# Runs of indirect scatters with a wait on GpSimd after every fourth

## The chip, the cores and the metric

The kernel runs on one core of a Trainium2 chip. A core has TensorE (matmul, PE in the profile, its weight loads PEld), VectorE (DVE), ScalarE (ACT), GpSimd (POOL) and SyncE (SP), which issues plain DMAs; all DMAs share 16 engines. The metric is the time of one execution on the device, in microseconds. Before the change it is 320.58 us, the median of three runs (319.81 to 322.14).

## The reference

A layer norm of `x` (16 rows of 512 tokens, 128 features each) feeds two branches, and both are added to `x`: a linear attention with a decay, and a mixture of four different experts of which each token uses two. Cut to what matters:

```python
xn = layernorm(x)
# attention
q, k, v = xn @ q_w, xn @ k_w, xn @ v_w              # 32 features each
scores = (q @ k.T) * decay ** max(diff - 1, 0) * (diff > 0)
attn = (scores @ v) @ o_w.T * out_scale
# experts
logits = xn @ router_w + router_b + load_balancer
rw, sel = top_k(logits, 2);  rw = softmax(rw)
e0 = silu(xn @ w1) * (xn @ w3) @ w2
e1 = gelu(((xn @ eq) @ wv @ wo) @ c1w) @ c2w         # with biases
e2 = two layer norms around a relu network, then gen_w
e3 = gelu(xn @ ml_w1) @ ml_w2
out = x + attn + sum(rw * chosen two experts)
```

All in float32.

## The kernel before

**Staging.** In the first stage the 16 rows of x are taken in six groups of 1, 1, 2, 4, 4 and 4 rows (`GROUPS`). For each row VectorE takes the moments, GpSimd makes the inverse standard deviation (`inverse`, L465, a `pow`), VectorE an offset (L470), ScalarE normalizes each 128-token chunk into a buffer `pay` (L475), TensorE transposes (L482), and so on through the projections and the attention. The sum of x and attention is stored to the output straight away by SyncE (`store`, L584).

**Lists.** Each token picks a pair of experts, and there are six pairs. A token's normalized row with its two weights and its own number (131 floats) is sent to the list of its pair in device memory, a table called `lists`. That is done by `Group.send`: an indirect DMA of GpSimd for each chunk of 128 tokens, 64 in all, each with 128 row numbers from a column of `idx`.

**Tiles.** In the second stage 21 tiles of at most 512 tokens of one pair (`LISTS`, `TURN`) are loaded from the lists (`load`, SyncE, L857, which waits for the last scatter of its group), transposed, passed through the two experts on TensorE with ScalarE and VectorE behind it, and summed into a buffer `o` (four of them; first written by `biases`, L885 and L887, and added to by `joined`, L939). Then `Tile.send` scatters each chunk of `o` with accumulation to the rows of the output whose numbers are in the tile's `to` (L871): 66 more indirect DMAs of GpSimd. Expert 2 has two layer norms, whose `pow` is on GpSimd too (`rstd_u`, `rstd_v`).

Both kinds of scatter go through one helper, `scatter`, and so appear on one line of the profile, L487. The kernel declares that two scatters into the same table do not depend on each other, so a scatter does not wait for the one before it.

**Order.** Every step is entered with `add(name, engine, us, fn, after, takes, rank)`: an assumed duration, what it must follow, which buffers it takes. `emit` then runs a small plan: it keeps for each engine the time from which it is free, picks the step that can start first (among those that start within 0.25 us of it on the same engine, the one of lowest rank), and issues its instructions. This fixes the order on TensorE, VectorE, ScalarE and SyncE; GpSimd's instructions follow the same plan through the helper `queued`. The plan chooses the PSUM banks and the buffers too. Names of steps that begin with `s` on GpSimd are the list scatters (`send0.0` and so on, 1.28 us by the plan), those with `X` the output scatters (1.87 us). A buffer that a scatter reads is free for others `LATE` us after the scatter's planned end.

At the end a count is taken that decides whether a slow path for overfull lists is run; with these inputs it is not.

Of the kernel before, what the change touches and what calls it, by code (L numbers as in the profile page):

```python
# [83 lines left out]
def decay_attention__plus__routed_experts(  # L84
# [10 lines left out]
    nc = tc.nc  # L95
# [17 lines left out]
        "h2T": 1, "z2T": 1, "o": 4,  # L113
    }

    LATE = {"x": 3.0, "o": 3.2, "pay1": 2.6, "pay2": 2.6}


# [25 lines left out]
    def queued(i, key=None):  # L144

        if queue["on"]:
            others = [q for q, k in queue["moving"] if k != key or key is None]
            for q in others or [queue["fixed"]]:
                if q is not None:
                    tc.add_manual_dep(i.ins, q, behind, reason="the order of the plan")  # L150
            if key:
                queue["moving"].append((i.ins.name, key))
            else:
                queue.update(fixed=i.ins.name, moving=[])
        return i
# [7 lines left out]
    PE, V, A, G, S = "PVAGS"  # L163
# [7 lines left out]
    def emit():  # L171
        free = dict.fromkeys("PVAGS", 0.0)
        slots = {kind: [()] * n for kind, n in ROOM.items()}
        slots["x"] = [(f"store{b}",) for b in range(ROOM["x"])]
        done, left = {}, {n: len(p[3]) for n, p in plan.items()}
        followers = {}
        for n, p in plan.items():
            for q, _ in p[3]:
                followers.setdefault(q, []).append(n)
        ready = [n for n in plan if not left[n]]  # L180
        while ready:
            starts = {}
            for n in ready:
                eng, us, fn, after, takes, rank, at = plan[n]
                t = max(at, free[eng])
                for q, lat in after:
                    if lat is None:
                        lat = 0.05 if plan[q][0] == eng else 0.2
                    t = max(t, done[q] + lat)
                for kind in {k for k, _ in takes}:  # L190
                    ends = sorted(
                        max((done[q] for q in s), default=-1.0) + LATE.get(kind, 0.2)
                        for s in slots[kind] if all(q in done for q in s)
                    )
                    count = sum(k == kind for k, _ in takes)
                    t = max(t, ends[count - 1]) if len(ends) >= count else None
                    if t is None:
                        break
                if t is not None:
                    starts[n] = t  # L200
            assert starts, f"no step can go on: {ready}"
            first = min(starts, key=starts.get)
            eng, soon = plan[first][0], starts[first] + 0.25
            n = min(
                (m for m in starts if plan[m][0] == eng and starts[m] <= soon),
                key=lambda m: (plan[m][5], starts[m]),
            )
            eng, us, fn, after, takes, rank, at = plan[n]
            for kind, users in takes:
                i = min(  # L210
                    (i for i, s in enumerate(slots[kind]) if all(q in done for q in s)),
                    key=lambda i: max((done[q] for q in slots[kind][i]), default=-1.0),
                )
                slots[kind][i] = (n, *users)
                given.setdefault((kind, n), []).append(i)
            running[0] = n
            fn()
            running[0] = None
            done[n] = free[eng] = starts[n] + us
            ready.remove(n)  # L220
            for m in followers.get(n, ()):
                left[m] -= 1
                if not left[m]:
                    ready.append(m)
        assert len(done) == len(plan), "a step waits for itself"
# [253 lines left out]
    def transposed(z, n, name):  # L479
# [2 lines left out]
            nc.tensor.transpose(pt[:, ts(c, P)], z(c), ident)  # L482
        return pt[:, : n * P]

    def scatter(o, src, index, n, key, **how):

        i = queued(nc.gpsimd.indirect_dma_start(  # L487
            out=o, out_offset=bass.IndirectOffsetOnAxis(ap=index, axis=0),
            in_=src, in_offset=None, bounds_check=n - 1, oob_is_err=False, **how,
        ), key)  # L490
        tc.add_to_no_dep_group(key, i.ins)
        tc.declare_no_dep(i.ins, group=key, reason="each row of the table is written once at most")
        if key == "lists":
            tc.declare_no_dep(i.ins, group="loads", reason="a tile is loaded when all its rows are there")

    def chosen(lg, n, pool, name):

        cin = pool.tile([P, NL, 1 + n], F32, tag=f"cin{n}", name=f"cin_{name}")  # L500
        pair = cin[:, :, 1:]
        dif = pool.tile([P, NL, n], F32, tag=f"dif{n}", name=f"dif_{name}")
        firsts = [(e, NE - 1 - e, e * (2 * NE - 1 - e) // 2) for e in range(NE - 1)]
        for e, m, at in firsts:
            nc.vector.tensor_tensor(
                dif[:, at : at + m], lg[:, e : e + 1].to_broadcast([P, m, n]), lg[:, e + 1 :], ALU.subtract
            )

        won = pool.tile([P, NL, n], F32, tag=f"won{n}", name=f"won_{name}", bufs=1)
        nc.vector.tensor_scalar(won, dif, 0.0, 0.5, ALU.is_ge, ALU.subtract)  # L510

        sums = pool.tile([P, NE, n], F32, tag=f"sums{n}", name=f"sums_{name}", bufs=1)
        w = lambda l: won[:, l, :]
        nc.vector.tensor_tensor(sums[:, 1, :], w(3), w(4), ALU.add)
        nc.vector.tensor_tensor(sums[:, 2, :], w(5), w(3), ALU.subtract)
        nc.vector.scalar_tensor_tensor(sums[:, 3, :], w(4), -1.0, w(5), ALU.mult, ALU.subtract)
        nc.vector.tensor_reduce(sums[:, 0, :], won[:, : NE - 1].rearrange("p l c -> p c l"), AX.X, ALU.add)
        nc.vector.tensor_tensor(sums[:, 1:], sums[:, 1:], won[:, : NE - 1], ALU.subtract)
        for e, m, at in firsts:
            nc.vector.tensor_tensor(  # L520
                pair[:, at : at + m], sums[:, e : e + 1].to_broadcast([P, m, n]), sums[:, e + 1 :], ALU.add
            )
        nc.vector.tensor_scalar(pair, pair, 1.5, None, ALU.is_gt)
        return cin, dif
# [173 lines left out]
    class Group:  # L698
# [52 lines left out]
        def send(s, k):  # L751
            scatter(lists, s.entry(k), s.idx[:, k : k + 1], NL * LR, "lists")
# [30 lines left out]
    for g, m in enumerate(GROUPS):  # L783
# [41 lines left out]
        n = NC * m  # L825
# [19 lines left out]
    class Tile:  # L845
# [138 lines left out]
        def send(s, c):  # L984
            scatter(rows_of_out, s.o[:, c, :], s.to[:, c : c + 1], B * T, "out", compute_op=ALU.add)
# [69 lines left out]
    with tc.manual_schedule(engines={E.PE, E.DVE, E.Activation, E.SP}):  # L1055
        queue["on"] = True
        emit()
        queue["on"] = False
# [29 lines left out]
    with tc.For_i(0, trips, 1) as i:  # L1088
# [20 lines left out]
        s = Dense(0, 3, 0, NC, "row")  # L1109
# [90 lines left out]
```

## Time and profile before

| | us |
|---|---|
| median of three runs (lowest, highest) | 320.58 (319.81, 322.14) |
| the profiled execution, in all | 373.55 |
| its span, first to last instruction | 371.5 |
| mean granted TensorE clock in it | 0.891 |
| GpSimd: 66 output scatters, busy | 103.0 (mean 1.561) |
| GpSimd: 64 list scatters, busy | 63.4 (mean 0.991) |
| GpSimd: 16 `pow` of the rows | 16.4 (mean 1.030) |

The profiled execution is longer than the timed ones. In a page's rows an engine's busy time is the time in which it worked on an instruction; a wait is idle time, and "<-" names what ended it. "issue" is idle time in which nothing that the profile shows was waited for. Instructions that issue DMAs end when the DMA has been described, not when its data have landed; landings are seen from the semaphores that the DMA raises. The slices of the page cut the span into 40 equal parts, with the busy share of each in tenths.

### The profile page before, as it was taken

How to read it: one execution, taken by the hardware profiler on the slowest of the kernel's cores; microseconds unless marked ns; L12 is line 12 of the kernel's file. 1: busy time of each engine (PE TensorE's matmuls, PEld its weight loads, DVE VectorE, ACT ScalarE, POOL GpSimd, SP SyncE). 2: the span in 40 equal slices, each digit the busy share in tenths (PEclk: the TensorE clock that was granted, in tenths of full speed). 3: DMA queues.
4: the chain of work that ended last, by engine and by line, in shares of the span. 5: the costliest groups of instructions: out<-in, count | busy, mean ns of one | idle time of the engine just before them, and what ended most of it. 6: DMA issues, size and time to landing. Idle time of an engine off the chain costs nothing. (4 is left out here: it accounts for less than half of the span.)

```text
span 371.5 us, 6510 instructions
## 1 busy us (share of the span) xinstructions
PE 307.8 (83%) x2194; PEld 234.0 (63%) x2194; DVE 208.7 (56%) x857; ACT 160.1 (43%) x358; POOL 203.6 (55%) x247
## 2 busy tenths in 40 slices
PE   1996979879300998996999999999999999999970
PEld 1854858455300695865468785775886877885860
DVE  4875657739230385731375964785858685475420
ACT  3784764336200613353253636144476266333420
POOL 5508773744775030277648884844364641784282
PEclk9986886668655599999899999999999999999995
DMA  7991174440251005021505362422133310442032
GB/s 225 283 205 50 39 211 117 119 119 8 78 167 43 1 17 156 9 75 36 79 8 66 28 89 21 66 21 36 12 55 58 43 16 1 69 48 19 3 33 23
DMA packets 34148, 25.60 MB, mean 69 GB/s; under 512 B 3648, under 2 KB 31552, under 8 KB 33984
## 3 DMA queue, kind: packets, MB, share of 16 engines
q0 software_dynamic: 11552, 8.50, 16.6%
q1 hardware_dynamic: 21840, 15.39, 16.4%
q10 hardware_dynamic: 720, 1.26, 1.0%
q8 instruction: 19, 0.31, 0.4%
q14 instruction: 17, 0.14, 0.1%
HBM read 11.65 MB, written 13.62 MB: 68 GB/s over the span
## 5 line engine op out<-in xcount | busy, mean ns | idle before, releaser
L487 POOL DMA_INDIRECT out_dram<-o,to x66 | 103.0, 1561 | 48.2 <-DVE o L939 33.1
L487 POOL DMA_INDIRECT lists<-pay,idx x64 | 63.4, 991 | 48.7 <-DVE sc L637 19.3
L939 DVE SCALAR_TENSOR_TENSOR o<-y_ps,xg,o 128x128 f32<-128x128 f32 x132 | 38.0, 345 | 51.7 <-PE y_ps L158 41.6
L158 PE MATMUL y_ps<-main_sb,h 128*128 128x128 f32 x456 | 55.4, 276 | 0.9 <-ACT h L916 0.9
L158 PEld LDWEIGHTS y_ps<-main_sb,h 128*128 128x128 f32 x456 | 53.7, 192 | 3.7 <-issue 1.2
L158 PE MATMUL proj_ps<-w_all,xnT 128*128 128x68 f32 x128 | 22.6, 344 | 19.3 <-ACT xnT L565 19.2
L158 PEld LDWEIGHTS proj_ps<-w_all,xnT 128*128 128x128 f32 x128 | 21.1, 254 | 21.0 <-ACT xnT L565 20.5
L158 PE MATMUL h_ps<-xT,main_sb 128*128 128x512 f32 (+2 forms) x88 | 34.1, 487 | 0.0
L916 ACT ACTIVATE h<-h_ps,cols_sb 128x512 f32<-128x512 f32 (+2 forms) x44 | 24.7, 579 | 17.2 <-PE h_ps L158 11.9
L902 DVE SCALAR_TENSOR_TENSOR th<-th,a_ps 128x384 f32<-128x384 f32 (+2 forms) x36 | 20.2, 566 | 18.8 <-ACT th L899 18.3
L158 PE MATMUL a_ps<-xT,w_sb 128*128 128x384 f32 (+2 forms) x72 | 29.9, 501 | 0.5 <-ACT xT L867 0.5
L916 ACT ACTIVATE h<-h_ps,b_e 128x512 f32<-128x512 f32 (+2 forms) x28 | 17.4, 626 | 29.7 <-PE h_ps L158 29.4
L158 PE MATMUL b_ps<-xT,w_sb 128*128 128x384 f32 (+2 forms) x72 | 28.5, 525 | 0.4 <-ACT xT L867 0.4
L899 ACT ACTIVATE th<-a_ps 128x384 f32<-128x384 f32 (+2 forms) x36 | 17.8, 499 | 24.9 <-PE a_ps L158 24.4
L475 ACT ACTIVATE pay<-x,off_x,rstd_x 128x128 f32<-128x128 f32 x64 | 26.1, 487 | 2.5 <-DVE off_x L470 2.5
L158 PEld LDWEIGHTS y_ps<-sw_w2h,h 128*128 128x128 f32 x224 | 26.1, 192 | 1.3 <-issue 0.5
L465 POOL TENSOR_TENSOR rstd_x<-ve_x,neg_half 128x4 f32<-128x4 f32 x16 | 16.4, 1030 | 18.9 <-DVE ve_x L460 15.2
L158 PE MATMUL y_ps<-sw_w2h,h 128*128 128x128 f32 x224 | 26.5, 275 | 0.0
L158 PE MATMUL h_ps<-xT,w_e 128*128 128x512 f32 (+2 forms) x56 | 25.2, 546 | 0.9 <-ACT xT L867 0.9
L465 POOL TENSOR_TENSOR rstd_u<-ve_u,neg_half 128x3 f32<-128x3 f32 (+2 forms) x8 | 8.2, 1022 | 28.2 <-DVE ve_u L460 28.2
L565 ACT COPY xnT<-xnT_ps 128x512 f32<-128x512 f32 x16 | 9.0, 583 | 32.8 <-remote 25.0
L907 DVE TENSOR_TENSOR h<-th,b_ps 128x384 f32<-128x384 f32 (+2 forms) x36 | 20.2, 568 | 2.2
(180 smaller groups left out, 506.5 us busy)
## 6 DMA issues: line engine op xcount, KB each, us to landing
x<-in_x_dram SPq DMA_DIRECT2D x16, 256.0 KB
out_dram<-x SPq DMA_DIRECT2D x16, 256.0 KB
xg<-lists SPq DMA_DIRECT2D x8, 262.0 KB
xg<-lists SPq DMA_DIRECT2D x8, 196.5 KB
main_sb<-in_main_dram SPq DMA_DIRECT2D x1, 1216.0 KB
out_dram<-o,to POOLq DMA_INDIRECT x66
lists<-pay,idx POOLq DMA_INDIRECT x64
lists<-none SPq DMA_DIRECT2D x6, 131.0 KB
```

Source lines behind the costliest of these rows:

```text
L158: nc.tensor.matmul(o, lhsT, rhs, start=start, stop=stop)
L465: queued(nc.gpsimd.tensor_tensor(rstd, ve, neg_half[:, :n], ALU.pow))
L475: nc.scalar.activation(o(c), v(c), AF.Identity, bias=off[:, c : c + 1], scale=rstd[:, c : c + 1])
L487: i = queued(nc.gpsimd.indirect_dma_start(out=o, out_offset=bass.IndirectOffsetOnAxis(ap=index, axis=0), in_=src, in_offset=None, bounds_c ...
L565: nc.scalar.copy(s.xnT, s.bank)
L899: nc.scalar.activation(s.th[i], s.ga[i], AF.Tanh, scale=0.5)
L902: nc.vector.scalar_tensor_tensor(s.th[i], s.th[i], 1.0, s.ga[i], ALU.add, ALU.mult)
L907: nc.vector.tensor_tensor(s.h0[:, i, :], s.th[i], s.gb[i], ALU.mult)
L916: nc.scalar.activation(getattr(s, key)[:, i, :], s.hb[key, i], func, bias=bias[:, i : i + 1])
L939: nc.vector.scalar_tensor_tensor(o, s.py[e][:, c, :], w(c), o, ALU.mult, ALU.add)
```

## The change

Three things are added. First, the plan counts the scatters of a run. After `RUN` = 4 scatters the next one may not start, in the plan, before the last one has landed, taken to be 2.6 us after the start of a list scatter and 3.6 us after that of an output scatter. A scatter that starts later than the landing of the one before begins a new run by itself. Second, where a scatter follows a full run with less than 0.3 us between, the column of row numbers that the last scatter used is noted in `rest`. Third, `scatter` then sets that column to zero with a memset on GpSimd ahead of the new scatter. The column is not used again; but since the scatter in flight reads it, the memset has to wait until that scatter is done, and GpSimd with it.

```diff
+    RUN, LANDS = 4, {"s": 2.6, "X": 3.6}
     LATE = {"x": 3.0, "o": 3.2, "pay1": 2.6, "pay2": 2.6}
...
         ready = [n for n in plan if not left[n]]
+        run, landed = 0, 0.0
         while ready:
             starts = {}
             for n in ready:
                 eng, us, fn, after, takes, rank, at = plan[n]
                 t = max(at, free[eng])
+                if eng == G and n[0] in LANDS and run >= RUN:
+                    t = max(t, landed)
...
+            if eng == G and n[0] in LANDS:
+                if run >= RUN and starts[n] < landed + 0.3:
+                    rest.append(last_index[0])
+                run = 1 if run >= RUN or starts[n] > landed else run + 1
+                landed = starts[n] + LANDS[n[0]]
             running[0] = n
             fn()
...
+    rest, last_index = [], [None]
+
     def scatter(o, src, index, n, key, **how):
+        if rest:
+            queued(nc.gpsimd.memset(rest.pop(), 0))
         i = queued(nc.gpsimd.indirect_dma_start(
...
             tc.declare_no_dep(i.ins, group="loads", reason="a tile is loaded when all its rows are there")
+        last_index[0] = index
```

## The prediction

> **What bounds the kernel now.** I read the page first (busy shares and the slices), then the windows by stage, then GpSimd's timeline, then the waits.
>
> ```profile
> PE 307.8 (83%) x2194; PEld 234.0 (63%) x2194; DVE 208.7 (56%) x857; ACT 160.1 (43%) x358; POOL 203.6 (55%) x247
> PE   1996979879300998996999999999999999999970
> POOL 5508773744775030277648884844364641784282
> PEclk9986886668655599999899999999999999999995
> ```
>
> One slice is 371.5 / 40 = 9.3 us. From slice 20 on TensorE is full; the hole in slices 10 to 12 (93 to 121 us) lies exactly where GpSimd is at 7, 7, 5. The windows give the stages (length, then busy of PE, PEld, DVE, ACT, POOL, then the granted clock):
>
> ```profile
> 92.00:120.00 28.00, 5.17 (x53) 4.37 (x52) 5.83 (x20) 3.50 (x9) 19.52 (x20) 0.57 0.33 98
> 200.00:240.00 40.00, 39.65 (x247) 31.14 (x246) 25.84 (x102) 18.45 (x37) 30.69 (x22) 1.00 0.45 57
> 240.00:280.00 40.00, 39.18 (x232) 29.83 (x231) 28.52 (x99) 21.73 (x45) 19.27 (x16) 1.00 0.23 29
> 280.00:320.00 40.00, 39.98 (x241) 30.56 (x240) 27.66 (x104) 22.06 (x46) 19.70 (x15) 1.00 0.24 35
> 345.00:372.00 27.00, 14.50 (x106) 13.68 (x105) 4.99 (x18) 5.31 (x13) 12.34 (x8) 0.82 0.22 21
> ```
>
> Three stages: routing and list scatters to about 173 us, expert tiles to 345 on a TensorE that is 98% busy, and a tail in which the last scatters go out one by one. In the tail GpSimd's queue ends the program. Its timeline (start, duration, what, idle before):
>
> ```profile
> 350.61 1.54 POOL L487 DMA_INDIRECT out_dram<-o,to  x1 [11.77 <-DVE o L939]
> 352.46 1.54 POOL L487 DMA_INDIRECT out_dram<-o,to  x1 [0.30 <-issue]
> 354.31 1.54 POOL L487 DMA_INDIRECT out_dram<-o,to  x1 [0.31 <-issue]
> 356.15 1.54 POOL L487 DMA_INDIRECT out_dram<-o,to  x1 [0.30 <-DVE o L939]
> ...
> 363.55 1.54 POOL L487 DMA_INDIRECT out_dram<-o,to  x1 [0.30 <-DMA out_dram<-o,to]
> ```
>
> The last join on VectorE starts at 359.39 and takes 0.61, so the last rows are ready at 360.0 and leave at 363.55: GpSimd is 3.5 us behind here.
>
> The profiled execution (373.55 us, 371.5 of it span) is 53 us longer than the median of 320.58, so the timed span is about 318.5. Where can 53 us come from? The rows of 200 to 345 are TensorE at work at full clock and cannot shrink. With the tail at 26.5 the timed run has 318.5 - 145 - 26.5 = 147 us for what the profile spreads over 200. Busy PE times granted clock, summed over my windows up to 200 us, is 128 us of full-clock work, and the first 20 us have 7.8 idle. That leaves about 11 us for every other idle and every slow-clock moment. The profile's own hole is larger than that:
>
> ```profile
> ACT xnT L565 <- remote: 25.0, 1, 25.0
> PE proj_ps L158 <- ACT xnT L565: 19.2, 3, 18.2
> ```
>
> Nine transposes end by 103.0 (modelled) and the semaphore that tells ScalarE of them moves only at 120.5. I conclude (an estimate, not shown by a trace) that the timed runs have little of this hole: their first stage is packed, and GpSimd in it is busier than 55% says.
>
> **The change, part by part.**
>
> *What it adds.* When the plan holds a fifth scatter less than 0.3 us after the fourth of a run has landed (2.6 us after its start for the lists, 3.6 for the output, by the plan), a memset of the previous scatter's index column is put ahead of it on GpSimd. It has to wait until that scatter has landed. The memset itself is small: the memsets `need<- 128x1` of the trace take 110 ns each, so with 21 of them 2.3 us. The wait is the cost.
>
> *Price of one rest.* Without it scatters of the lists follow at 1.28 us (0.97 + 0.30), of the output at 1.85 (1.54 + 0.30). By the semaphore counts of the trace a list scatter has landed 2.1 to 2.3 us after its start, an output one about 3.3 (3.0 at least), and the end of the program shows the same:
>
> ```profile
> SPq L1088 <- DMA out_dram<-o,to: 5.0, 2, 3.4
> ```
>
> That is SyncE's wait from 363.48 for the scatter of 363.55. A rest thus makes the next start come at landing + 0.1 + 0.11 memset + 0.2 (the gap that this timeline shows ahead of a scatter after another instruction): lists 2.1 + 0.4 = 2.5, +1.25 us; output 3.3 + 0.4 = 3.7, +1.85 us. The Trainium skill ("DMA: Bandwidth & Descriptors", section "Anatomy of one DMA — SWDGE (gpsimd) path") says that one such DMA costs about 2.0 us fixed plus bytes / 436e3, mostly waiting for the receipt of the write; it speaks against the change, since each rest exposes just that. By it a 64 KB output scatter lands after 2.15 us, and a rest costs 2.15 + 0.4 - 1.85 = 0.7. The row says 3.3: these scatters add to memory. I take the row; by the rule the eleven output rests below would sum to 7.7 instead of 20.4 us.
>
> *How many.* Laying the rule of the diff over the start times of this trace gives 21 rests: 10 among the list scatters (five of them in the run of 21 from 90.9 to 116.5 us) and 11 among the output scatters. Sum on GpSimd: 10 x 1.25 + 11 x 1.85 = 33 us. In the packed timed run the runs are longer; 16 + 16 is the most that 64 and 66 scatters allow, 50 us.
>
> *Where it is paid.* Tail: the run of eight starts anew at 350.61 (the scatter before was at 337.30), so there is one rest after the fourth. 356.15 + 3.7 = 359.85 where 358.00 was: **+1.85 us, in full**, because nothing follows but GpSimd.
>
> Before the tail GpSimd is occupied for 203.6 us plus 28 us of issue gaps, 232 us, 73% of 318.5; with the rests 265 us, 83%. Behind a waiting memset stand the next scatters and, if the plan put them later, the `pow` of L465 (0.7 to 1.1 us), for which VectorE's L470, then ScalarE's L475, then TensorE's transposes wait; SyncE's loads of `xg` wait for the last list scatter of their group; VectorE's first write of an `o` buffer (four of them) waits for the scatters that read it, and the second product of a tile is planned behind that write. The plan knows of the rest (with constants 0.3 to 0.5 us above the landings measured) and puts other GpSimd work into it where there is some.
>
> Two places are tight. From 154.7 to 183.4 GpSimd is continuously at work (twelve scatters for the lists, then six for the output): four rests, 3 x 1.25 + 1.85 = 5.6 us, and a pause of 6.8 us follows in the profile. From 190.2 to 227.7 it is continuous again: four rests, 7.4 us, with pauses of 3.9, 3.5 and 5.1 us after it; two `pow` of the second layer norm lie in it. From below the exposed part is nothing (TensorE at 98% has other tiles' products to go on with; this cover is the four `o` and the eight banks, gone if a tile's output is held more than one tile longer), from above 5.6 + 7.4 = 13 us. The nearest row for a wait of this kind in the profile is
>
> ```profile
> DVE off_x L470 <- POOL rstd_x L465: 5.1, 3, 3.9
> ```
>
> so delays of GpSimd reach the others sometimes, by up to 3.9 us. I take one such delay, 3.5 us. The list rests (12.5 us, 20 at the most) delay the last group's loads; ahead of these TensorE has twelve tiles, so nothing is taken for them, and up to 4 us are kept for the range.
>
> A second rule bears on the price of a delay: "TensorE: Matmul & The Clock Gate", section "Part 1: The HAM clock gate (the "warmup" mystery)", has the clock halve after some 3.4 us of idleness. The 200 to 345 windows show 1.00 and no such gap. By the row a 3.5 us delay costs 3.5; by the rule, were it one gap of TensorE, up to 1.7 more for the cold restart. I keep that for the upper end.
>
> *What it moves.* The plan is made anew with other times on GpSimd, so the order of all engines and the choice of banks and buffers may shift. Nothing in the trace prices that; I allow 2 us either way.
>
> *Sum:* 1.85 + 3.5 = 5.4 us, on the profiled execution 379. Both parts lie in stages that do not depend on the hole, so I carry them to the median unscaled: 320.6 + 5.4 = 326.0.
>
> **The rivals.**
>
> A (forecast, 57%): tail plus a delay or two in the packed part, 323.9 to 332; likeliest 326.
>
> B (27%, the case of no change among them): only the tail pays; all else is hidden behind TensorE, 322.4, with the new order 320 to 323.8. For it: three windows at 98% while POOL is at half. It includes that the change does not do what it says: if the memset does not have to wait for the landing, 21 x 0.3 us on an idle engine, no change.
>
> C (11%, faster): the hole is made by the run of 21 scatters, and is in the timed runs too; rests cut it up. For it: late semaphores of TensorE are found in the trace at 75, 91, 93, 103 and 167 to 173 us, within scatter runs each time, and almost none after 176. Against it: the run of twelve from 316.9 to 337.3 and the other output runs go along with a full TensorE, and the timed run has room for no more than about 11 us of it. If half of these go, 5.5 - 1.85 give 317. It decides once the stage before 173 us gains more than the 5.1 us that tail and a 1% threshold ask for.
>
> D (5%, much slower): GpSimd becomes the bound; of 33 to 50 us half is exposed: 337 to 345.
>
> **How the numbers follow.** A difference below 1% (3.2 us) is what a measurement of this kernel cannot tell from no change. Faster than 317.4: C alone, and its better half plus a lucky plan, 0.11. Within: B with C's weak side, 0.27. Slower: A and D, 0.62. The predicted time is A's, 326.0. The range leaves out C's better part below 318 and the part of A and D above 333: about one in ten on each side.
>
> **What would show it.** GpSimd's timeline after: memsets of `to` and `idx`, about 20 to 30, each with a scatter start 2.5 (lists) or 3.7 us (output) after the fourth; a tail of 4 + 4 scatters with 3.7 us between; POOL's waits on DMA of 30 to 45 us in total; PE below 98% in the stage before the tail, with waits that go back to `o` or `rstd`. The page's hole at 93 to 121 us may go in the profiled run without the median moving; if the median falls with it, C was right and my reading of the 53 us wrong. Fewer than ten rests, or a tail without one, would make the forecast too high.

## The result and the profile after

| us | before | after |
|---|---|---|
| median (lowest, highest), four runs each | 321.36 (319.81, 323.04) | 346.89 (346.18, 348.41) |
| the profiled execution of after | | 346.18, span 344.1 |
| ratio, 95% interval | | 1.080 [1.073, 1.087] |

The change costs 25.5 us, 8%. The forecast was 326.0, the range ended at 333; only the rival given 5%, "GpSimd becomes the bound; … half is exposed: 337 to 345", comes near it.

In some series of runs the kernel before takes about 321 us and in others about 374: the profile that the prediction read is of the second kind, the result and the experiments b, c and d are of the first, a and e of the second, and each is compared with the before of its own series. The kernel before was profiled once more in the first kind (run c0_before, 319.02 us), and that profile stands beside the one of after here.

The page of after, busy times and then the 40 slices of 8.6 us:

```profile
PE 299.7 (87%) x2194; PEld 225.1 (65%) x2194; DVE 206.4 (60%) x857; ACT 160.8 (47%) x358; POOL 205.1 (60%) x270
PE   1996996899999499978999989999999999999930
POOL 4606883758544566566666877768666425663562
PEclk9978999699999879998999999999999999999985
```

The page of before in 319 us (slices of 7.9 us):

```profile
PE 291.9 (92%) x2194; PEld 223.0 (70%) x2194; DVE 207.8 (66%) x857; ACT 159.6 (50%) x358; POOL 203.8 (64%) x247
PE   1899998899999999999999999999999999999940
PEclk9999999999999999999999999999999999999985
```

GpSimd did 1.3 us more work with its 23 memsets. TensorE is where the time went: its digits fall below 9 before slice 24, counted from 0 (the 4 in slice 13 is at 112 to 120 us), and PEclk has a 6 and two 7s there. The first 7, at 17 to 26 us, lies ahead of the first rest and is not its doing: the page of d1, a run below that has no waits, shows a 7 and a 5 between 24 and 40 us. Before has no 7 or less in either row between its first slice and its tail: the hole of the earlier page is not in a run of 319 us. The windows of after (from:to, length, then busy time and count of PE, PEld, DVE, ACT and POOL, granted clock, DMA share, GB/s) give the places:

```profile
61.00:65.00 4.00, 3.79 (x36) 2.54 (x40) 3.48 (x17) 1.97 (x7) 2.69 (x4) 0.50 0.35 58
65.00:69.00 4.00, 4.00 (x56) 2.66 (x52) 3.69 (x27) 1.81 (x5) 3.42 (x4) 0.88 0.35 114
...
100.00:120.00 20.00, 14.69 (x112) 10.71 (x107) 11.82 (x38) 5.81 (x13) 10.65 (x14) 0.93 0.31 91
120.00:126.00 6.00, 6.00 (x23) 4.51 (x23) 1.99 (x5) 3.20 (x7) 3.96 (x4) 0.66 0.27 80
...
155.00:159.00 4.00, 4.00 (x13) 2.59 (x13) 2.44 (x9) 1.95 (x5) 1.62 (x3) 0.61 0.18 16
...
225.00:320.00 95.00, 93.99 (x564) 73.34 (x564) 61.83 (x215) 46.35 (x96) 52.66 (x42) 1.00 0.29 36
```

From 225 to 320 us TensorE is 99% busy at full clock. Before that, it stood still three times after the start stage: 57.53 to 61.21, 114.57 to 119.73 and 152.52 to 154.82 us (from the ends and starts of its matmuls), 11.1 us together, and each time the granted clock in the windows behind is lower: 0.50, 0.66, 0.61.

The waits of after (in total, how many, the longest):

```profile
POOL idx L501 <- DMA lists<-pay,idx: 22.6, 11, 4.9
POOL to L501 <- DMA out_dram<-o,to: 19.1, 12, 1.9
DVE off_u L480 <- POOL rstd_u L475: 14.5, 5, 7.5
DVE off_x L480 <- POOL rstd_x L475: 10.1, 7, 4.2
DVE o L901 <- DMA out_dram<-o,to: 9.4, 6, 4.4
PE zuT_ps L492 <- ACT z L485: 7.8, 3, 5.2
DVE off_v L480 <- POOL rstd_v L475: 7.1, 5, 3.0
```

And of before in 319 us (its lines have numbers lower by 10):

```profile
DVE off_x L470 <- POOL rstd_x L465: 3.5, 6, 1.2
DVE off_u L470 <- POOL rstd_u L465: 1.5, 2, 0.9
DVE off_v L470 <- POOL rstd_v L465: 0.5, 2, 0.3
```

GpSimd waits 41.7 us in its 23 memsets; such a wait is called a rest from here on. VectorE's waits for a `pow` of GpSimd rise from 5.5 to 31.7 us, and a wait for an output buffer `o` appears that before does not have. One rest is followed here through the engines, with the rests ahead of the other two gaps and the tail around it (start, duration, engine, line, what, idle before and what ended it):

```profile
50.30 0.97 POOL L502 DMA_INDIRECT lists<-pay,idx  x1 [0.30 <-issue]
56.23 0.10 POOL L501 MEMSET idx<- 128x1 uint32 x1 [4.95 <-DMA lists<-pay,idx]
57.05 0.96 POOL L502 DMA_INDIRECT lists<-pay,idx  x1 [0.72 <-issue]
...
59.31 1.05 POOL L475 TENSOR_TENSOR rstd_x<-ve_x,neg_half 128x4 f32<-128x4 f32 x1
...
60.39 0.16 DVE L480 SCALAR_TENSOR_TENSOR off_x<-mv_x,rstd_x 128x4 f32<-128x4 f32 x1 [4.21 <-POOL rstd_x L475]
...
108.07 0.97 POOL L502 DMA_INDIRECT lists<-pay,idx  x1 [0.30 <-issue]
111.30 0.17 DVE L470 TENSOR_SCALAR ve_u<-mv_u 128x3 f32<-128x3 f32 x1
112.40 0.10 POOL L501 MEMSET idx<- 128x1 uint32 x1 [3.36 <-DMA lists<-pay,idx]
113.22 0.97 POOL L502 DMA_INDIRECT lists<-pay,idx  x1 [0.72 <-issue]
...
117.05 0.97 POOL L502 DMA_INDIRECT lists<-pay,idx  x1 [0.30 <-issue]
118.04 0.91 POOL L475 TENSOR_TENSOR rstd_u<-ve_u,neg_half 128x3 f32<-128x3 f32 x1
118.98 0.16 DVE L480 SCALAR_TENSOR_TENSOR off_u<-mv_u,rstd_u 128x3 f32<-128x3 f32 x1 [7.51 <-POOL rstd_u L475]
119.18 1.26 ACT L485 ACTIVATE z<-uv,off_u,rstd_u 128x128 f32<-128x128 f32 x3 [8.11 <-DVE off_u L480]
119.73 0.86 PE L492 MATMUL zuT_ps<-ident,z 128*128 128x128 f32 x2 [5.16 <-ACT z L485]
...
153.12 0.92 POOL L475 TENSOR_TENSOR rstd_u<-ve_u,neg_half 128x3 f32<-128x3 f32 x1
...
154.82 1.25 PE L492 MATMUL zuT_ps<-ident,z 128*128 128x128 f32 x3 [2.30 <-ACT z L485]
...
326.56 1.54 POOL L502 DMA_INDIRECT out_dram<-o,to  x1 [0.30 <-DVE o L955]
329.83 0.10 POOL L501 MEMSET to<- 128x1 uint32 x1 [1.73 <-DMA out_dram<-o,to]
330.65 1.55 POOL L502 DMA_INDIRECT out_dram<-o,to  x1 [0.73 <-DVE o L955]
```

The variance `ve_u` is ready at 111.5. Its `pow` stands in GpSimd's queue behind a rest and four scatters and starts at 118.04; VectorE has stood still for 7.5 us, ScalarE for 8.1, TensorE for 5.2. The rest before 112.40 is one of 23, and the scatter after it comes 5.15 us after the fourth, not 2.5. The other two gaps have the same cause. At 57 us a `pow` of the rows (59.31) stands behind the rest that ends at 56.23 and two scatters; VectorE waits for it with `off_x`, which stands ahead of the `sc` that TensorE needs. At 152 us a `pow` (153.12) stands behind a rest that ends at 148.78 and three scatters. All three rests are among the list scatters.

### The profile page after: what moved, and what is told of

The parts are those of the page before. It is cut to its first block, busy times and chain, and to the rows that moved or that the text cites. A ratio compares the mean times of both kernels' runs of the same rounds, so it can differ in the third digit from the quotient of the medians.

```text
span 344.1 us, 6529 instructions
## 1 busy us (share of the span) xinstructions
PE 299.7 (87%) x2194; PEld 225.1 (65%) x2194; DVE 206.4 (60%) x857; ACT 160.8 (47%) x358; POOL 205.1 (60%) x270
## 5 line engine op out<-in xcount | busy, mean ns | idle before, releaser
L160 PEld LDWEIGHTS y_ps<-main_sb,h 128*128 128x128 f32 x456 | 54.8, 196 | 2.6 <-issue 1.4
L160 PE MATMUL h_ps<-xT,main_sb 128*128 128x512 f32 (+2 forms) x88 | 32.9, 487 | 0.0
L160 PE MATMUL b_ps<-xT,w_sb 128*128 128x384 f32 (+2 forms) x72 | 26.8, 499 | 0.0
L160 PEld LDWEIGHTS h_ps<-xT,main_sb 128*128 128x128 f32 x88 | 15.9, 191 | 8.2 <-issue 3.3
L160 PE MATMUL proj_ps<-w_all,xnT 128*128 128x68 f32 x128 | 19.9, 315 | 1.1 <-ACT xnT L581 1.0
L901 DVE TENSOR_SCALAR o<-rows_sb,xg 128x128 f32<-128x128 f32 x66 | 15.1, 294 | 9.4 <-DMA out_dram<-o,to 9.4
L160 PEld LDWEIGHTS proj_ps<-w_all,xnT 128*128 128x128 f32 x128 | 18.4, 226 | 2.7 <-ACT xnT L581 2.5
```

The lines of the kernel that those rows point to most:

```text
L160: nc.tensor.matmul(o, lhsT, rhs, start=start, stop=stop)
L901: nc.vector.tensor_scalar(o, bias, w(c), None, ALU.mult)
```

## The experiments

**The order alone, the memset alone, the waits.** Three kernels cut the change up. Plan only: after's order, no memset. No wait: the memsets are there, but write a tile of their own, so they wait for nothing. Old order: before's order on every engine, with waiting memsets put in by the same rule (24 of them), the plan knowing nothing of the rests. They ran first in the series of 374 us:

```diff
 # a1_plan_only, b1_plan_only
-                    rest.append(last_index[0])
+                    pass
 # a2_no_wait, b2_no_wait
+    spare = const.tile([P, 1], U32, tag="spare", name="spare")
...
-            queued(nc.gpsimd.memset(rest.pop(), 0))
+            rest.pop()
+            queued(nc.gpsimd.memset(spare, 0))
 # a3_old_plan, b3_old_plan
-                if eng == G and n[0] in LANDS and run >= RUN:
-                    t = max(t, landed)
```

> The kernel before, once more, for a second profile. If the hole of 93 to 121 us belongs to this order of work (its long run of list scatters), it is there again and the profiled execution is near 373 us. If it was an accident of one execution, or of being profiled, the profile now is near the timed 321 us and shows where GpSimd and TensorE stand without it. Time: 321 within 1%.

> The plan of the change, with no memset, so no wait. Every engine's order is that of the changed kernel, less 23 memsets on GpSimd. Theory W (the waits on GpSimd cost the time): as before, 318 to 325. Theory O (the new order costs it): 335 to 347. Theory D (the memset's own cost and the longer gap ahead of the scatter after it): 318 to 325.

> As the change, but each of the 23 memsets writes a column of its own that no scatter reads, so it waits for no landing. Same order on all engines. Theory W: little of the 25 us is left; 23 times 0.6 us (0.1 memset, 0.7 gap instead of 0.3) are 14 us of GpSimd's time, partly hidden: 321 to 330. Theory D: 338 to 347. Theory O: 347.

> The order of the kernel before on every engine, with the memsets put in by the same rule (24 of them), so the plan knows nothing of the waits. Theory W: at least the changed kernel's time, 345 to 360. Theory O: 321 to 326.

| run, before 374.33 beside them | us | ratio [95%] |
|---|---|---|
| a0_before | 374.27 | 0.997 [0.993, 1.002] |
| a1_plan_only | 377.19 | 1.015 [1.004, 1.026] |
| a2_no_wait | 375.08 | 1.007 [1.003, 1.012] |
| a3_old_plan | 367.38 | 0.983 [0.961, 1.005] |

The page of a0_before has the hole again:

```profile
PE   1998869779211999997899999999999999999950
```

and that of a3_old_plan, with the same order and a wait after every fourth scatter, does not:

```profile
PE   1998898779798699999867899999999999999940
```

So in the series of 374 us the hole goes when rests cut up the run of scatters, as the third rival said; but the interval of a3 takes in 1, so a gain is not shown. The comparison that answers for the result is the same four again, in a series where before takes 320.73:

> The changed kernel once more. The kernel before took 321 us beside the changed kernel, and 374 beside the first four experiments, on another chip, so there are two conditions, and the stall of TensorE within runs of scatters seems to be the second. Theory S (the stall depends on the condition, and the rests break it): where the kernel before takes 374, the changed one takes 345 to 355 and is faster; where it takes 321, the changed one takes 347. Theory N (the rests do nothing against the stall): 347 where before is 321, and over 390 where it is 374.

> The plan of the change with no memset, again, beside the changed kernel. Where the kernel before takes 321: theory W (the waits cost) 318 to 325, theory O (the order costs) 335 to 347. Where it takes 374: 377 as before.

> Memsets that wait for nothing, in the changed order, again. Where the kernel before takes 321: theory W 321 to 330; theory D (the memset and its gap cost) 338 to 347. Where it takes 374: 375 as before, so a memset without a wait does not break the stall.

> The order of the kernel before with the waits, again. Where the kernel before takes 321: theory W 345 to 360, theory O 321 to 326. Where it takes 374: 367 as before.

| run, before 320.73 beside them | us | ratio [95%] |
|---|---|---|
| b0_after | 346.30 | 1.077 [1.067, 1.087] |
| b1_plan_only | 323.98 | 1.010 [1.008, 1.013] |
| b2_no_wait | 325.52 | 1.014 [1.004, 1.024] |
| b3_old_plan | 363.79 | 1.130 [1.120, 1.141] |

The new order costs 3.3 us, the waiting 346.3 - 325.5 = 20.8; the 1.5 us left for the memsets without their wait lie within the interval of b2. In an order that does not know of them 24 waits cost 43. That the plan knows of the rests therefore saves much; it does not cause the loss.

Two rows also bear on the third rival: old order takes 367.38 us in the series of 374 and 363.79 here, 3.6 apart, where before, plan only and no wait are 50 to 54 apart. With waits, the two kinds of series nearly agree. A memset that waits for nothing does not do that (a2).

b0 and b2 have the same order on every engine but GpSimd's memsets, so each matmul can be compared with itself. How much later it starts with the waits (worked out from the start times in both traces; up to 50 us they differ by -2.5 to 0.1):

| at us, with the waits | 50 | 61 | 70 to 110 | 121 | 130 to 150 | 160 | 180 to 200 | 210 | from 220 |
|---|---|---|---|---|---|---|---|---|---|
| later by us | -0.6 | 3.2 | 4 | 10.6 | 13.4 | 16.0 | 16.7 | 18.6 | 19.6 |

Steps at 61, 121 and 160 us carry most of it, one of 3 us between 200 and 220 the rest, and the tail adds 2.2. The first three are TensorE's gaps in b0 (3.50, 6.65 and 1.70 us; b2 has none over 0.93 us from 30 us on) and the lower clock behind each: between 60 and 68, 120 and 126, and 155 and 163 us, TensorE's busy time in windows of 4 to 6 us times the share of the clock withheld (0.50, 0.09; 0.50; 0.27, 0.16) is 6.0 us. Gaps and clock make 17.9 of the 19.6. The waits of b2 that correspond to those of after are:

```profile
DVE off_x L480 <- POOL rstd_x L475: 3.6, 5, 1.7
DVE off_v L480 <- POOL rstd_v L475: 3.3, 4, 1.1
DVE o L903 <- DMA out_dram<-o,to: 3.2, 2, 1.8
DVE off_u L480 <- POOL rstd_u L475: 2.7, 4, 1.0
```

With the same instructions in the same order, VectorE waits for no `pow` longer than 1.7 us there: it is the landing, not the order of the queue, that makes VectorE stand 7.5 us in after (9.0 in b0).

**The profile of before in 319 us, and each kind of rest alone.**

```diff
 # c1_lists_only ("s"), c2_out_only ("X" in its place)
-                if run >= RUN and starts[n] < landed + 0.3:
+                if n[0] == "s" and run >= RUN and starts[n] < landed + 0.3:
```

> The kernel before, for a profile where it takes 321 us (if the chip is one of those). Then the hole of 93 to 121 us is absent, and GpSimd's run of list scatters goes on without TensorE standing still. Where it takes 374, the hole is there for the third time.

> The changed order on every engine, but only the 11 memsets ahead of list scatters are there; the 12 ahead of output scatters are left out. The two kernels with and without waits in this order stood at 346.3 and 325.5 us, so 20.8 us are to be shared out. From the lag of TensorE between these two profiles (4 us by 63 us, 13 by 125, 16 by 160 us, when the last list scatter goes out): theory P (the waits cost by what stands behind them on GpSimd when TensorE needs it) 338 to 342. If the output scatters' waits matter most (through the four buffers o and the tail), 328 to 332.

> The changed order, with only the 12 memsets ahead of output scatters. Theory P: 330 to 334, of which 2.2 are the tail. If the output scatters matter most: 340 to 344. If both parts are hidden when alone (GpSimd has room for one, not for two): both near 326 to 330.

| run, before 321.20 beside them | us | ratio [95%] | over b2, no wait (325.5) |
|---|---|---|---|
| c1_lists_only, 11 waits | 338.17 | 1.053 [1.047, 1.060] | 12.7 |
| c2_out_only, 12 waits | 331.02 | 1.030 [1.024, 1.036] | 5.5 |

The two make 18.2 of the 20.8 (b2's series had a before 0.5 us faster), and the larger one is that of the list rests, for which the prediction took nothing. The gaps of TensorE show which rests make them: c1 has all three (4.02, 5.16 and 1.84 us), c2 has none over 1.24 us from 32 us on. What c2 loses comes from 155 us on, 3.9 us up to 205 and the tail's 2.2. c0_before shows the stage of the hole, here with a full TensorE at full clock while GpSimd sends lists at 78% busy:

```profile
92.00:120.00 28.00, 28.00 (x193) 20.79 (x186) 16.75 (x52) 13.46 (x26) 21.91 (x23) 1.00 0.34 104
```

A long run of scatters alone does not stop TensorE in this series.

**Is it the `pow` behind the waits?** In c3 the 16 `pow` of expert 2 are replaced by a product on VectorE, so its rows are scaled by other numbers; all waits stay. d1 is the same without the waits.

```diff
+        if name[0] == "x":
+            queued(nc.gpsimd.tensor_tensor(rstd, ve, neg_half[:, :n], ALU.pow))
+        else:
+            nc.vector.tensor_tensor(rstd, ve, neg_half[:, :n], ALU.mult)
```

> The changed kernel with all 23 waits, but the pow of expert 2's two layer norms (16 of the 32 on GpSimd) is left out; VectorE makes a product in its place, at the same place of the order, so expert 2's output is not the reference's and the tokens' routing is. Theory P: the largest jumps of the lag are where rstd_u and rstd_v stand behind a waiting memset (+6.4 us at 120, +1.5 at 156, +3 at 181 to 218), so 332 to 338. If GpSimd is the bound by its sum: it loses 16 us of work and 16 gaps, and the time falls by no more than a few us without the waits being the reason: 340 to 344.

> The twin of the kernel without expert 2's pow on GpSimd (339.9 us), with memsets that wait for nothing; expert 2's norms are products as there. If the pow behind the waits was the way of about 7 us and the rest goes by other ways, this twin stands at 325, as with the pow, and the waits cost 15 here against 20.8. If the pow away is a gain of its own (16 us less of GpSimd's work): 318 to 321, and the waits cost as much as before, 20.

c3 took 339.93 (1.058 [1.053, 1.064]), d1 323.39 (1.009 [1.005, 1.012]). Without those `pow` the waits cost 16.5 instead of 20.8: they account for 4.3 us. More was expected if the `pow` were the whole way (332 to 338). Matmul by matmul against d1 the step at 120 us is gone (c3 is 3.4 us late at 70, 3.0 at 120), but from 130 on it is 7.1 to 7.6 late and from 180 on 13.1 to 13.2, up to the tail. Its waits say where the delay goes instead:

```profile
POOL idx L504 <- DMA lists<-pay,idx: 24.4, 11, 5.6
POOL to L504 <- DMA out_dram<-o,to: 20.9, 12, 1.9
DVE o L904 <- DMA out_dram<-o,to: 12.1, 3, 5.2
DVE to L890 <- DMA xg<-lists: 4.5, 1, 4.5
```

GpSimd's lateness itself remains, and what feels it is the next in line: in c3 the gap of TensorE at 125 us (2.09) follows VectorE's wait for the load of a tile (`xg`, 4.5 us, until 125.68), and the gap at 171 us (2.55) its wait for a buffer `o` that a scatter still reads (3.5 us, until 171.98). The lag does not grow after 180 us, so GpSimd's sum of work is not the bound there.

**The size of the rest, their number, more buffers.**

```diff
 # d2_true_price, d3_run_8
-    RUN, LANDS = 4, {"s": 2.6, "X": 3.6}
 # d2_true_price
+    RUN, LANDS = 4, {"s": 3.6, "X": 4.1}
 # d3_run_8
+    RUN, LANDS = 8, {"s": 2.6, "X": 3.6}
 # d4_six_o
-        "h2T": 1, "z2T": 1, "o": 4,
+        "h2T": 1, "z2T": 1, "o": 6,
```

> The change with LANDS at 3.6 and 4.1 us instead of 2.6 and 3.6, near what a rest costs in the trace (next start 3.2 to 4 us after the fourth for the lists, 4.1 for the output); 28 memsets instead of 23. If the plan's wrong price is the loss: 328 to 336. If the number of waits is: 346 or more, by five waits 348 to 354.

> Runs of eight: 11 memsets instead of 23. If every wait costs its share: 321 + 25 x 11/23 = 333. If only a few places cost (a pow behind a wait at 60 and 120 us, the tail), it depends on where the waits fall: 326 to 340; the tail then has none, 2.2 less.

> The change with six buffers o instead of four. If the output scatters' share goes through o: 340 to 343. If it goes through pow and tail alone: 345 to 348. The list scatters' part (13 to 16 us) stays in either case.

| run, before 320.52 beside them | us | ratio [95%] |
|---|---|---|
| d2_true_price, 28 waits | 347.22 | 1.084 [1.080, 1.088] |
| d3_run_8, 11 waits | 334.17 | 1.042 [1.037, 1.047] |
| d4_six_o, 23 waits | 338.08 | 1.056 [1.052, 1.060] |

With larger landings in the plan the kernel is no faster, 26.7 us over before with 28 waits against 25.5 with 23. Since five waits were added too, d2 does not show whether the better price gained something that they took back. Half as many waits cost about half, 13.6 for 11 (1.2 us each, against 1.1), d3's own order included. Two more buffers give about 8 us back (8.2 against b0), and the wait of VectorE for them is nearly gone:

```profile
DVE off_u L480 <- POOL rstd_u L475: 14.4, 5, 6.9
DVE o L901 <- DMA out_dram<-o,to: 1.1, 1, 1.1
```

The wait for `pow` is not. But d4 also changes the order: the first two gaps are there (3.68 and 4.61 us), the third is gone, which in c1 the list rests make alone. So the 8 us may hold a gain that has nothing to do with the output buffers' waits. That was tried with before, and with the kernel without waits, at six buffers; the series turned out to be one with before at 374.01:

> The kernel before with six buffers o, no waits. If the buffers are a gain of their own: 313 to 317, better than both kernels. If they only ease the waits: 319 to 322.

> The changed kernel with six buffers o and memsets that wait for nothing. If the buffers only ease the waits: 324 to 326, and the waits cost 12 to 14 with six instead of 20.8. If the buffers are a gain of their own: 317 to 320, and the waits cost as much as with four.

e1 took 368.39 (0.981 [0.974, 0.988]), e2 371.19 (0.999 [0.995, 1.003]). Whether six buffers gain anything where before takes 321 stays open, and with it how much of the 8 us is the waits'. No version was found that beats 321 us.

## Why the prediction was wrong

**The step that failed** is the one on the list rests, "ahead of these TensorE has twelve tiles, so nothing is taken for them", together with "I take one such delay, 3.5 us" for the whole kernel. The list rests alone cost 12.7 us (c1). Work in store did not help, since the order on TensorE is fixed when the program is written, and its next instruction is the one that waits: at 114.6 us the transposes `zuT`, behind ScalarE, VectorE and a `pow` in GpSimd's queue. The prediction named this very chain as what stands behind a waiting memset. It then priced it by a row of waits from a profile in which no scatter waited for a landing, and took one delay where the lags show four. The upper end, 13 us, came from two places: the last twelve list scatters with the output scatters behind them, and a later run of output scatters. The third gap, the smallest, lies in the first of these; the two larger ones, at 57 and 114 us, lie among earlier list scatters, where nothing was looked for.

**The number of rests** was right (23; "about 20 to 30" was to be seen). **Their price** was too low, "lists 2.1 + 0.4 = 2.5 … output 3.3 + 0.4 = 3.7" from the fourth scatter to the next. In after it is 3.2 to 6.8 us for the lists and 4.1 to 4.2 for the output. Over the 1.28 and 1.85 us without a rest that sums to 29.1 + 27.4 = 56.5 us, where 33 was forecast. The gap after a memset that has waited (0.66 to 0.74 instead of 0.2 us) is one part, later landings of list scatters the other. But the price of a rest on GpSimd is not the loss: of 56.5 us, 20.8 were paid at the end. With half as many waits (d3) the loss was about half.

**The tail** was forecast at 1.85 in full and costs 2.2: right, and the longer gap after the memset makes the difference. **The new order**, "2 us either way", costs 3.3. The memsets' own issue stood only in the price of a rest, not in the sum; the 1.5 us measured for it are not clear of noise.

**The clock.** The row shown in the prediction had 1.00 everywhere, so a delay of 3.5 us was taken as 3.5. The rule of the Trainium skill ("TensorE: Matmul & The Clock Gate", section "Part 1: The HAM clock gate (the "warmup" mystery)"), by which the clock halves after an idle window of about 3.4 us, was kept for the upper end. It belonged in the sum: in b0 the half clock came with all three gaps and cost 6.0 us. By the rule only the two gaps as long as that window (3.50 and 6.65 us) would bring it, an estimated 1.7 us each, 3.4 together. The traces go further: the third gap, 1.70 us in b0 and 2.30 in after, is shorter than the window and was followed by 0.73 and 0.61 all the same.

**The cover.** The condition "gone if a tile's output is held more than one tile longer" named the right place: VectorE's wait for `o` grows from 3.2 us (b2) to 9.8 (b0; 9.4 in after), and with six buffers it goes. By how many tiles an output was held was not measured, and how much of d4's 8 us that is stays open, as said.

**The rivals.** The 53 us between the profile and the median were read rightly: c0 has no hole, and so C's gain has no object where the result was measured. Its mechanism fits a3, which takes 367 us in the series of 374; after itself did not run in such a series, so whether the change would gain there stays open. B fell with c1. D came nearest in size; the cause that it names, that GpSimd becomes the bound, is not what the runs show: from 225 to 320 us TensorE is 99% busy again, and GpSimd is busy for 60% of the span. GpSimd is late at a few points, and a fixed order makes TensorE wait at each.

## What to carry to other kernels

A wait put into a queue that works in order is to be priced by what stands behind it and by how soon someone needs that, not by its own length or by the busy share of its engine. Where the other engines' order is fixed too, one late small operation (here a `pow` of 0.9 us) can stop the fullest of them, whatever other work there is, and each gap is to be counted with the slow clock behind it. Taking that operation out of the queue (c3) moved most of the delay to the next thing that waits, so it is the lateness that has to go. An average of 98% busy says that the engine had no gaps under the old timing; it does not say that it can bridge new ones.

## What the runs showed of the hardware

In after a list scatter that is followed by a rest had landed 2.3 to 5.9 us after its start, and the long landings are those with much DMA traffic around them. The windows from the fourth scatter's start to the memset, for two long and two short ones (length first, DMA share and GB/s last):

```profile
50.30:56.23 5.93, 4.84 (x99) 4.07 (x98) 5.60 (x32) 2.73 (x9) 0.98 (x2) 1.00 0.71 214
...
108.07:112.40 4.33, 4.33 (x38) 4.07 (x36) 3.33 (x14) 2.10 (x4) 0.97 (x1) 1.00 0.63 179
...
132.14:134.48 2.34, 2.34 (x23) 2.34 (x22) 1.13 (x4) 1.20 (x2) 0.96 (x1) 1.00 0.17 57
...
146.38:148.78 2.40, 2.40 (x12) 1.63 (x12) 2.26 (x10) 0.60 (x1) 0.97 (x2) 1.00 0.17 56
```

All four list landings beyond 3 us have a DMA share of 0.63 to 0.72, the seven below it 0.16 to 0.40. The share alone does not decide it: in d2 two list scatters landed after 3.3 and 3.5 us at shares of 0.15 and 0.14. The output scatters' landings hardly move in after, 3.27 to 3.47 us at shares from 0.22 to 0.65; one of d2 took 4.5 us at 0.35.

A scatter starts 0.30 us after another scatter, and 0.66 to 0.74 us after a memset that has waited for a landing (after). After a memset that waited for nothing it starts 0.14 to 0.19 us later (b2), so about 0.5 us of each rest come after the landing.

The half clock also follows gaps of TensorE that are well under 3.4 us. In the thirteen traces of the series of 321 us, from 40 us on and ahead of the tail, all 26 gaps of 1.70 to 6.65 us were followed by a granted clock of 0.50 for 3.4 to 10.2 us (setting in within 3.5 us of the gap's end at the latest), and the four gaps of 1.23 to 1.44 us were not. In the series of 374 us there are exceptions: in e1 a gap of 3.28 us at 173 us was not followed by it.

What decides between 321 and 374 us for one and the same program was not found. In the series of 374 us TensorE stops within the long run of list scatters (in a0_before from 93.9 to 101.2 and from 106.6 to 120.3 us); in the series of 321 us, with the same scatters, it doesn't.
